# ScalarE makes the scattered token copies six ahead, with their extra column, in the expert part of an adaLN–Mamba–MoE block

## The chip, the cores and the metric

The kernel runs on one core of one Trainium2 chip. The metric is the device time of one execution in microseconds (us); the kernel before has a median of 2375.14 us over three runs (2374.47 to 2376.8). Engines are named as the profile names them: PE (TensorE, matrix products), DVE (VectorE), ACT (ScalarE), POOL (GpSimd), and SP (SyncE), whose queue issues most of the DMA transfers. [...]

## The reference

Two sequences of 2048 tokens with 256 channels pass through an adaptive layer norm and a bidirectional Mamba block, and then through a mixture of experts. Only the second half matters here:

```
h = layernorm(x) * (1 + cb) + sb
scores = softmax(h @ gate_w.T)                    # 8 experts
top_vals, idx = top_k(scores, 2)                  # two experts per token
xs = h[:, None, :] * weights[:, :, None]          # two scaled copies of each token
y = sum over experts e of mask_e * ((silu(xs@w1[e].T+b1[e]) @ w2[e].T + b2[e]) * (xs@w3[e].T + b3[e]))
z = silu(h @ sw1.T) * (h @ sw2.T) @ sw3.T         # shared expert, every token
out = x + gb * (y + z)
```

All arrays are float32. There are 2 x 2048 tokens and two copies of each, so 8192 rows of 256 numbers go to the experts.

## The kernel before, in words

The program has four stages. Up to about 1897 us of the profiled execution it runs the two Mamba directions. From about 1921 to 2076 us, which I call phase A, it opens the layer norm of both batches ("front" units), picks the experts of every token ("choose" and "rank" units on DVE), runs most of the shared expert (matmul groups `pg` and `pz` on PE), and scatters the first batch's token copies. From 2076 to about 2347 us, the expert stage, it runs 40 expert tiles of 256 rows. The last stage, to 2395 us, finishes the shared expert of the second batch and stores the output.

**How copies reach their experts.** For each batch there are 16 column blocks `j` and two ranks `n`, so 32 copies, each of 128 tokens on 128 partitions and 257 columns. ACT writes 256 columns: the normalised tokens times their expert weight (L1173). POOL writes the extra column 257 (L1176): a number, from `homes[b]`, from which the row is later computed to which the expert's result must return. POOL then issues an indirect DMA (L1177), which writes the 128 rows to the places `slots[b]` of the DRAM tensor `xs`. The copies live in a pool of eight buffers, so the ACT instruction that makes copy k has to wait until the DMA of copy k-8 has landed. `homes[b]` and `slots[b]` come from `route(b)` on DVE, whose last instruction of interest is L1145.

**Phase A's order** is written by hand: a list of 37 steps `k`, each with one shared-expert unit and some front units beside it. `follow(generator)` advances a generator by one yield. From step 17 on each step advances the first batch's scatter generator twice.

**The expert stage.** For tile i the SP queue loads three weight matrices, the biases and the tile's 256 rows `xg` from `xs` (`load_tile`, L1225 to L1229), three tiles ahead, each with four buffers. PE does `qh` (first product), `q` (third matrix), turns the next tile in (`qgT`), turns the last tile's result out (`qyT`), and does `q` again (second matrix, which needs `hT`). ACT applies silu to `qh` and writes `hT` (L1301), writes the third product with its bias (`x`, L1304), and copies the turned result to `outs` (L1273). DVE copies the turned-in tile `gT` (L1253) and multiplies the two products (L1311). At the end of tile i comes `sides(i)`: up to tile 7 it advances the second batch's scatter generator four times; from tile 9 (`NF` is 9) it sends finished tiles, two in a tile while there are several, each by two indirect DMAs from POOL (L1281) to the DRAM tensor `ys`.

**What orders scatters against loads.** Tiles 0 to 8 hold only rows of the first batch, so their loads are declared independent of the second batch's scatters. From tile 9 on the load of a tile must wait for all scatters that stand before it in the program, and a scatter that stands after a load must wait for that load. `load_tile(9)` stands in tile 6, before that tile's `sides`.

Of the kernel before, what the change touches and what calls it, by code (L numbers as in the profile page):

```python
# [8 lines left out]
F32 = mybir.dt.float32  # L9
AF = mybir.ActivationFunctionType  # L10
# [5 lines left out]
P = 128  # L16
NB, T, C = 2, 2048, 256
NJ = T // P
# [7 lines left out]
JC = TC // P  # L26
# [10 lines left out]
NF = -((E * (TS - 1) - 2 * T) // TS)  # L37
# [6 lines left out]
def kernel(  # L44
# [4 lines left out]
    nc = tc.nc  # L49
# [11 lines left out]
        out=flip, in_=flip, compare_op=ALU.not_equal, fill=1.0,  # L61
# [12 lines left out]
    xs_d = dram.tile([NT * TS, C + 1], F32, tag="xs", name="xs")  # L74
# [20 lines left out]
    x1s, xhs, mods = {}, {}, {}  # L95
# [47 lines left out]
    with tc.tile_pool(name="mw", bufs=1) as mw, tc.tile_pool(name="mw2", bufs=2) as mw2, \  # L143
# [44 lines left out]
        weights, state, ready, xns, accs = {}, {}, {}, {}, {}  # L188
# [359 lines left out]
        places = {}  # L548
# [307 lines left out]
        for s in range(NST + 4 + SPC):  # L856
            i, k = divmod(s, SPC)
# [41 lines left out]
            if i < NCH + 1:  # L899
# [3 lines left out]
                if k == 8 and 2 <= i < 2 + NB:  # L903
                    v = xs_d.rearrange("(p n) f -> p (n f)", p=P).rearrange("p (m k) -> p m k", k=NX)
                    n = slice((i - 2) * C // 2, C + 1 if i > 2 else C // 2)
# [30 lines left out]
    with tc.tile_pool(name="fw", bufs=1) as fw, tc.tile_pool(name="f1", bufs=1) as f1, \  # L936
# [44 lines left out]
        spare = fw.tile([P, 1], F32, tag="spare", name="spare")  # L981
# [5 lines left out]
        homes = [fw.tile([P, 2, NJ], F32, tag=f"home{b}", name=f"home{b}") for b in range(NB)]  # L987
# [8 lines left out]
        for v, pattern, base, each in ((filled, [[0, E], [TS, NK]], 0, 0), (tiles, [[1, NT], [0, NQ]], 0, 0),  # L996
# [4 lines left out]
            n = v.shape[1] * v.shape[2]  # L1001
# [3 lines left out]
        picks = {}  # L1005
# [68 lines left out]
                nc.vector.tensor_reduce(sc[:, n, js], got, AX.X, ALU.add)  # L1074
            yield

        slots, owners, left = {}, {}, {}

        def route(b):

# [80 lines left out]
        def apart(i, own, others, reason):  # L1161

            i = getattr(i, "ins", i)
            for group in others:
                tc.declare_no_dep(i, group=group, reason=reason)
            tc.add_to_no_dep_group(own, i)

        def scatter(b):
            sc = picks[b][1]
            for j in range(NJ):  # L1170
                for n in range(2):
                    v = f4.tile([P, C + 1], F32, tag="xs", bufs=8, name=f"xs{b}_{j}_{n}")
                    nc.scalar.activation(v[:, 0:C], xhs[b, j // JC][:, j % JC, :], AF.Copy,  # L1173
                                         scale=sc[:, n, j:j + 1])

                    nc.gpsimd.tensor_copy(v[:, C:C + 1], homes[b][:, n, j:j + 1])  # L1176
                    i = nc.gpsimd.indirect_dma_start(  # L1177
                        out=xs_d[:, :], in_=v, in_offset=None,
                        out_offset=bass.IndirectOffsetOnAxis(ap=slots[b][:, n, j:j + 1], axis=0))
                    apart(i, f"scatter{b}", (f"scatter{b}", f"load{b}"), "each writes rows of its own")  # L1180
                    yield

        def shared(b, q):

# [34 lines left out]
        def load_tile(i):  # L1219

            e = nc.sync.value_load(owners[i >= NF][0:1, i:i + 1], min_val=0, max_val=E - 1)
            ws = f4.tile([P, 3, KC, H], F32, tag="we", bufs=4, name=f"we{i}")
            xg = f4.tile([P, 2, C + 1], F32, tag="xg", bufs=4, name=f"xg{i}")
            for n, src in enumerate((w1, w3, w2)):
                nc.sync.dma_start(out=ws[:, n, :, :], in_=src[bass.ds(e, 1), :, :]  # L1225
                                  .rearrange("o (k p) h -> p (o k) h", p=P))
            bs = f4.tile([P, 3, KH], F32, tag="bs", bufs=4, name=f"bs{i}")
            nc.sync.dma_start(out=bs, in_=b123[:, :, bass.ds(e, 1), :].rearrange("p n o k -> p n (o k)"))
            d = nc.sync.dma_start(out=xg, in_=tiled(xs_d[i * TS:(i + 1) * TS, :]))  # L1229
            if i < NF:  # L1230
                apart(d, "load1", ("scatter1",), "full of the first batch's tokens")
            loaded[i] = ws, bs, xg

        def lin(ws, n, src, name):
            ps = bank(name).rearrange("p (m t) -> p m t", m=2)
            for m in range(KH):
                for k in range(KC):
                    nc.tensor.matmul(ps[:, m, :], ws[:, n, k, m * P:(m + 1) * P], src[:, k, :],  # L1238
                                     start=(k == 0), stop=(k == KC - 1))
            return ps  # L1240
# [8 lines left out]
        def turned_in(i):  # L1249
            xg = loaded[i][2]  # L1250
            ps = turn_tile(xg[:, :, 0:C], f"qgT{i}")
            gT = f2.tile([P, KC, TS], F32, tag="gT", name=f"gT{i}")
            nc.vector.tensor_copy(gT, ps)  # L1253
            nc.vector.scalar_tensor_tensor(xg[:, :, C], xg[:, :, C], float(i * TS), empty[:, 0, :],
                                           ALU.add, ALU.add)
            homeward[i] = f4.tile([P, 2], U32, tag="home", bufs=12, name=f"home{i}")
            nc.vector.tensor_copy(homeward[i], xg[:, :, C])
            return gT
# [27 lines left out]
        def expert_tiles(sides):  # L1286


            for i in range(3):
                load_tile(i)  # L1290
            gT, x3 = turned_in(0), None
            follow(routes[1])
            for i in range(NT):
                if i + 3 < NT:
                    load_tile(i + 3)
                ws, bs, _ = loaded.pop(i)
                hT = f2.tile([P, KH, TS], F32, tag="hT", name=f"hT{i}")
                y3 = f2.tile([P, KC, TS], F32, tag="x3", name=f"x3{i}")
                ps = lin(ws, 0, gT, f"qh{i}")
                for m in range(KH):  # L1300
                    nc.scalar.activation(hT[:, m, :], ps[:, m, :], AF.Silu, bias=bs[:, 0, m:m + 1])  # L1301
                ps = lin(ws, 1, gT, f"q3{i}")
                for m in range(KC):
                    nc.scalar.activation(y3[:, m, :], ps[:, m, :], AF.Identity, bias=bs[:, 2, m:m + 1])  # L1304
                if i + 1 < NT:
                    gT = turned_in(i + 1)
                if x3 is not None:
                    turned_out(i - 1, x3)
                ps = lin(ws, 2, hT, f"q2{i}")
                for m in range(KC):  # L1310
                    nc.vector.scalar_tensor_tensor(y3[:, m, :], ps[:, m, :], bs[:, 1, m:m + 1],  # L1311
                                                   y3[:, m, :], ALU.add, ALU.mult)
                x3 = y3
                sides(i)
            turned_out(NT - 1, x3)
# [27 lines left out]
        def store(b, q):  # L1343
            nc.sync.dma_start(out=tiled(out[b, q * TC:(q + 1) * TC, :]), in_=x1s[b, q])
# [5 lines left out]
        def part(b, q, n):  # L1350
            if n == LOAD:
                load_front(b, q)
            else:
                next(fronts[b, q], None)
# [3 lines left out]
        def unit(f):  # L1358
            e = f() if f else None
            while emptied:  # L1360
                emptied.pop(0)()
            if e:
                emptied.append(e)

        def follow(f):

            return next(f, 0) != 0
# [12 lines left out]
        def interleaved(keys):  # L1380

            units, due = [], []
            for k in keys:
                units += hidden[k][:2] + due + hidden[k][2:]
                due = result[k]
            return units + [None] + due
# [13 lines left out]
        scatters, routes = [scatter(0), scatter(1)], [route(0), route(1)]  # L1400
        for k, f in enumerate(interleaved([(0, 0), (0, 1), (0, 2), (0, 3), (1, 0), (1, 1)])):
            for p in beside.get(k, ()):
                part(*p)
            if k == 8:
                for v, w in iotas:
                    nc.vector.tensor_copy(v.rearrange("p a b -> p (a b)"), w)
            if k in (14, 16, 33):
                follow(routes[k // 33])
            unit(f)
            if k > 16:  # L1410
                for _ in range(2):
                    follow(scatters[0])
        while emptied:
            emptied.pop(0)()
        while follow(scatters[0]):
            pass

        twos = {}

        def sides(i):  # L1420
            for _ in range(4):
                follow(scatters[1])
            if i == 1:
                follow(routes[1])
            if i >= NF:
                for _ in range(2 if len(made) > 1 else 1):
                    send()
            for q in range(NTC):
                if i == N0 + 2 + 3 * q:
                    twos[q] = combine(0, q, fetch(0, q))  # L1430
                if N0 + 4 + 3 * q <= i <= N0 + 6 + 3 * q and not follow(twos[q]):
                    store(0, q)

        expert_tiles(sides)
        while made:
            send()
# [70 lines left out]
```

## Time and profile before

| what | value |
|---|---|
| median of three runs | 2375.14 us |
| profiled execution, its own time | 2396.49 us |
| span of the profiled execution | 2394.8 us |
| busy over the span: PE, DVE, ACT, POOL | 81%, 85%, 67%, 79% |
| expert stage up to tile 9 (2076 to 2140 us) | PE busy 61.96 of 64 us |
| tiles 10 and 11 (2140 to 2175 us) | PE busy 16.18 of 35 us |
| rest of the expert stage (2175 to 2347 us) | PE busy 171.90 of 172 us |

The profile is one execution, 21.35 us longer than the median of the runs without one. A timeline line gives the start in us, the duration in us, engine, source line, operation, output and input tiles, how many instructions are merged into the line, and in brackets how long the engine stood idle before it and what ended that idle time. `L1301` is line 1301 of the kernel. A line with x8 covers eight instructions.

### The profile page before, as it was taken

How to read it: one execution, taken by the hardware profiler on the slowest of the kernel's cores; microseconds unless marked ns; L12 is line 12 of the kernel's file. 1: busy time of each engine (PE TensorE's matmuls, PEld its weight loads, DVE VectorE, ACT ScalarE, POOL GpSimd, SP SyncE). 2: the span in 40 equal slices, each digit the busy share in tenths (PEclk: the TensorE clock that was granted, in tenths of full speed). 3: DMA queues.
4: the chain of work that ended last, by engine and by line, in shares of the span. 5: the costliest groups of instructions: out<-in, count | busy, mean ns of one | idle time of the engine just before them, and what ended most of it. 6: DMA issues, size and time to landing. Idle time of an engine off the chain costs nothing. (4 is left out here: it accounts for less than half of the span.)

```text
span 2394.8 us, 29909 instructions
## 1 busy us (share of the span) xinstructions
PE 1941.8 (81%) x9320; PEld 1333.1 (56%) x9320; DVE 2034.5 (85%) x2743; ACT 1599.9 (67%) x3345; POOL 1893.1 (79%) x1083
## 2 busy tenths in 40 slices
PE   5466878797978788887979788887876699987999
PEld 2133555554646555554556465555555555776885
DVE  5489999989999999999999999999999978622244
ACT  5557787768778787878787777878775344442331
POOL 0267898989999999999999999999999613564331
PEclk9678988888999899998889898999987899998999
DMA  4344448585444545445455445454446331466683
GB/s 161 107 156 159 145 166 199 189 213 182 152 168 164 166 153 185 156 159 168 141 171 172 159 153 170 155 160 160 145 166 217 101 121 43 146 200 197 215 291 144
DMA packets 230403, 393.70 MB, mean 164 GB/s; under 512 B 68162, under 2 KB 159810, under 8 KB 230244
## 3 DMA queue, kind: packets, MB, share of 16 engines
q1 hardware_dynamic: 222900, 371.30, 48.6%
q0 software_dynamic: 6912, 18.92, 2.1%
q8 instruction: 73, 1.20, 0.2%
q10 hardware_dynamic: 432, 1.58, 0.2%
q14 instruction: 86, 0.70, 0.1%
HBM read 340.27 MB, written 51.46 MB: 164 GB/s over the span
## 5 line engine op out<-in xcount | busy, mean ns | idle before, releaser
L461 POOL TENSOR_TENSOR db<-du,B 128x1024 f32<-128x1024 f32 x452 | 1061.2, 2366 | 18.2 <-DMA B<-bcs 10.8
L505 POOL TENSOR_TENSOR db<-h,C 128x1024 f32<-128x1024 f32 x252 | 597.4, 2371 | 65.8 <-issue 53.5
L480 ACT ACTIVATE da<-dt,w_a 128x512 f32<-128x512 f32 x904 | 594.7, 688 | 76.4 <-DVE dt L345 45.8
L527 PE MATMUL y<-ident,db 128*128 128x128 f32 x4096 | 566.5, 286 | 39.6 <-POOL db L505 37.2
L527 PEld LDWEIGHTS y<-ident,db 128*128 128x128 f32 x4096 | 503.7, 149 | 161.5 <-issue 101.1
L494 DVE TENSOR_TENSOR_SCAN da<-da,hl,db 128x512 f32<-128x512 f32 x460 | 562.8, 1268 | 4.9 <-POOL db L461 3.7
L494 DVE TENSOR_TENSOR_SCAN h<-da,hl,db 128x512 f32<-128x512 f32 x444 | 540.0, 1263 | 15.3 <-ACT da L480 15.3
L500 DVE TENSOR_TENSOR db<-da,C 128x512 f32<-128x512 f32 x460 | 292.1, 676 | 22.0 <-DMA C<-bcs 14.5
L281 PE MATMUL psc<-xp,w_conv 128*128 128x512 f32 x512 | 236.4, 605 | 10.2 <-ACT xp L270 6.4
L264 PE MATMUL psx<-xT,w_in 128*128 128x512 f32 x256 | 155.4, 727 | 102.7 <-ACT hl L515 90.1
L399 PE MATMUL psz<-w_in,xT 128*128 128x512 f32 x256 | 151.3, 723 | 56.3 <-ACT bT L362 36.3
L1281 POOL DMA_INDIRECT ys<-outs,home x80 | 76.7, 959 | 122.1 <-ACT outs L1273 112.3
L351 POOL TENSOR_TENSOR du<-dt,xc 128x512 f32<-128x512 f32 x64 | 81.3, 1271 | 98.4 <-DVE dt L345 98.4
L281 PEld LDWEIGHTS psc<-xp,w_conv 128*128 128x128 f32 x512 | 94.3, 194 | 108.3 <-issue 96.5
L298 PE MATMUL psd<-xc,w_x 128*48 128x512 f32 x128 | 96.8, 927 | 68.0 <-ACT hl L515 47.5
L427 PE MATMUL pso<-w_out,yg 128*128 128x256 f32 x512 | 118.6, 385 | 23.5 <-ACT e L321 22.2
L264 PEld LDWEIGHTS psx<-xT,w_in 128*128 128x128 f32 x256 | 49.8, 223 | 156.8 <-ACT hl L515 112.1
L1253 DVE COPY gT<-qgT 128x512 f32<-128x512 f32 x40 | 27.6, 691 | 113.3 <-PE qgT L947 82.7
L1301 ACT ACTIVATE hT<-qh,bs 128x256 f32<-128x256 f32 x80 | 33.5, 469 | 130.9 <-issue 75.9
L515 ACT COPY hl<-da 128x1 f32<-128x1 f32 x460 | 61.6, 157 | 87.6 <-DVE db L500 84.7
L427 PEld LDWEIGHTS pso<-w_out,yg 128*128 128x128 f32 x512 | 95.7, 192 | 39.1 <-ACT e L321 25.5
L1195 PE MATMUL pg<-fxT,s 128*128 128x512 f32 x256 | 115.3, 602 | 1.6 <-DVE hs L1201 0.7
(251 smaller groups left out, 3123.7 us busy)
## 6 DMA issues: line engine op xcount, KB each, us to landing
C<-bcs SPq DMA_DIRECT2D x256, 512.0 KB
B<-bcs SPq DMA_DIRECT2D x226, 512.0 KB
we<-in_w_dram SPq DMA_DIRECT2D x120, 256.0 KB
acc<-acc SPq DMA_DIRECT2D x32, 512.0 KB
xg<-xs SPq DMA_DIRECT2D x40, 257.0 KB
xn<-xn SPq DMA_DIRECT2D x16, 512.0 KB
two<-ys SPq DMA_DIRECT2D x16, 512.0 KB
xs<-blank SPq DMA_DIRECT2D x1, 5160.0 KB
```

What stands on the lines that cost most here:

```text
L264: nc.tensor.matmul(ps, w["in"][:, k, d * P:(d + 1) * P], v["xT"][:, k, :], start=(k == 0), stop=(k == KC - 1))
L281: nc.tensor.matmul(ps, w["conv"][:, d, k, :], v["xp"][:, d, k:k + TC], start=(k == 0), stop=(k == 3))
L298: nc.tensor.matmul(ps[:RK + 2 * NS, :], w["x"][:, d, :], v["xc"][:, d, :], start=(d == 0), stop=(d == ND - 1))
L399: nc.tensor.matmul(ps, v["xT"][:, k, j * P:(j + 1) * P], w["in"][:, k, DI:2 * DI], start=(k == 0), stop=(k == KC - 1))
L427: nc.tensor.matmul(ps[:, n, :], v["yg"][:, d, n * P:(n + 1) * P], wo[:, d, :], start=(d == 0), stop=(d == ND - 1))
L461: nc.gpsimd.tensor_tensor(db, bc(ready[i]["du"][:, d, :], NG), live["B", s // 2], ALU.mult)
L480: nc.scalar.activation(da[n], ready[i]["dt"][:, d, :], AF.Exp, scale=w["a"][:, d, m:m + 1])
L494: nc.vector.tensor_tensor_scan(h[n], da[n], x[n], hl[:, d, m:m + 1], ALU.mult, ALU.add)
L500: nc.vector.tensor_tensor(live["db", s][:, n, :], h, live["C", s // 2][:, n, :], ALU.mult)
L505: nc.gpsimd.tensor_tensor(live["db", s], live.pop(("h", s)), live["C", s // 2], ALU.mult)
L527: nc.tensor.matmul(ys["y"][j // 2][:, j % 2, d % 2 * P:(d % 2 + 1) * P], src[:, j * P:(j + 1) * P], ident, is_transpose=True, start=(first ...
L1195: nc.tensor.matmul(ps, s12[:, n, k, m * P:(m + 1) * P], xTs[b, q][:, k, :], start=(k == 0), stop=(k == KC - 1))
```

## The change

The scatter generator is split. It first makes six copies and yields after each; then, for each k, it makes copy k+6, writes the extra column of copy k on ACT, and issues the scatter of copy k from POOL. The extra column's POOL copy becomes an ACT copy of 128x1, and POOL gets a memset of a spare 128x1 tile in its place. In phase A the first batch's generator is advanced from step 14. After phase A the second batch's generator is advanced six times, and six times more at the start of the expert stage, ahead of tile 0. Sends begin in tile 7. The eight buffers stay.

```diff
         def scatter(b):
-            sc = picks[b][1]
-            for j in range(NJ):
-                for n in range(2):
-                    v = f4.tile([P, C + 1], F32, tag="xs", bufs=8, name=f"xs{b}_{j}_{n}")
-                    nc.scalar.activation(v[:, 0:C], xhs[b, j // JC][:, j % JC, :], AF.Copy,
-                                         scale=sc[:, n, j:j + 1])
-
-                    nc.gpsimd.tensor_copy(v[:, C:C + 1], homes[b][:, n, j:j + 1])
-                    i = nc.gpsimd.indirect_dma_start(
...
-                    yield
+            sc, ready = picks[b][1], []
+            places = [(j, n) for j in range(NJ) for n in range(2)]
+
+            def make(j, n):
+                v = f4.tile([P, C + 1], F32, tag="xs", bufs=8, name=f"xs{b}_{j}_{n}")
+                nc.scalar.activation(v[:, 0:C], xhs[b, j // JC][:, j % JC, :], AF.Copy,
+                                     scale=sc[:, n, j:j + 1])
+                ready.append(v)
+
+            for k in range(AHEAD):
+                make(*places[k])
+                yield
+            for k, (j, n) in enumerate(places):
+                if k + AHEAD < len(places):
+                    make(*places[k + AHEAD])
+                v = ready.pop(0)
+                nc.scalar.copy(v[:, C:C + 1], homes[b][:, n, j:j + 1])
+
+                nc.gpsimd.memset(spare, 0.0)
+                i = nc.gpsimd.indirect_dma_start(
...
+                yield
...
             follow(routes[1])
+            for _ in range(AHEAD):
+                follow(scatters[1])
             for i in range(NT):
...
-            if k > 16:
+            if k > 13:
                 for _ in range(2):
                     follow(scatters[0])
...
         while follow(scatters[0]):
             pass
+        for _ in range(AHEAD):
+            follow(scatters[1])
...
-            if i >= NF:
+            if i >= NF - 2:
                 for _ in range(2 if len(made) > 1 else 1):
                     send()
```

`AHEAD` is 6.

More of the change, by code (lines that the diff above doesn't have):

```diff
@@ L1075, in front @@
             yield
-        slots, owners, left = {}, {}, {}
+        slots, owners, left, AHEAD = {}, {}, {}, 6
         def route(b):
@@ L1168, in scatter @@
         def scatter(b):
-            sc = picks[b][1]
-            for j in range(NJ):
-                for n in range(2):
-                    v = f4.tile([P, C + 1], F32, tag="xs", bufs=8, name=f"xs{b}_{j}_{n}")
-                    nc.scalar.activation(v[:, 0:C], xhs[b, j // JC][:, j % JC, :], AF.Copy,
-                                         scale=sc[:, n, j:j + 1])
[L1176 to L1180, printed above, removed]
-                    yield
+            sc, ready = picks[b][1], []
[15 more added lines that the diff above has]
+                i = nc.gpsimd.indirect_dma_start(
+                    out=xs_d[:, :], in_=v, in_offset=None,
+                    out_offset=bass.IndirectOffsetOnAxis(ap=slots[b][:, n, j:j + 1], axis=0))
+                apart(i, f"scatter{b}", (f"scatter{b}", f"load{b}"), "each writes rows of its own")
+                yield
         def shared(b, q):
```

## The prediction

> **What bounds the kernel now.** I read the table of busy time by stage first, to see where PE does not work.
>
> ```profile
> 2076.00:2140.00 64.00, 61.96 (x328) 54.48 (x327) 26.85 (x77) 34.59 (x81) 35.30 (x60) 1.00 0.75 220
> 2140.00:2175.00 35.00, 16.18 (x62) 13.10 (x62) 3.61 (x10) 4.30 (x10) 24.71 (x46) 0.71 0.54 165
> 2175.00:2347.00 172.00, 171.90 (x898) 152.18 (x896) 62.06 (x149) 63.24 (x140) 60.65 (x113) 0.99 0.75 235
> ```
>
> The columns are the stretch, its length, busy time of PE, PE's weight loads, DVE, ACT and POOL, then granted clock, DMA share and GB/s. The expert stage is bound by PE except between 2140 and 2175 us. What stops it there stands in the timelines of SP, POOL and PE.
>
> ```profile
> 2124.23 0.38 SPq L1229 DMA_DIRECT2D xg<-xs  x1
> 2134.67 0.38 SPq L1229 DMA_DIRECT2D xg<-xs  x1
> 2145.63 0.38 SPq L1229 DMA_DIRECT2D xg<-xs  x1
> ```
>
> ```profile
> 2127.84 0.98 POOL L1177 DMA_INDIRECT xs<-xs,slot  x1 [4.99 <-ACT xs L1173]
> 2138.34 0.98 POOL L1177 DMA_INDIRECT xs<-xs,slot  x1 [4.96 <-ACT x L1304]
> ```
>
> ```profile
> 2148.65 1.12 PE L947 MATMUL qgT<-ident,xg 128*128 128x128 f32 x4 [4.76 <-DMA xg<-xs]
> ...
> 2150.41 3.62 PE L1238 MATMUL q<-hT,we 128*128 128x256 f32 x8
> ...
> 2173.40 3.78 PE L1238 MATMUL q<-hT,we 128*128 128x256 f32 x8 [10.79 <-ACT hT L1301]
> ```
>
> Loads of tiles 9, 10, 11 and the last eight scatters take turns: each waits for the other, 10.4 us a round where a tile takes PE 6.05 us (`qh` starts at 2083.61 and 2089.67). So tile 11's rows come 4.76 us late.
>
> The second stall, up to 2173.40, is of another kind.
>
> ```profile
> 2156.44 8.42 SPq L1225 DMA_DIRECT2D we<-in_w_dram  x3
> ```
>
> ```profile
> ACT hT L1301 <- remote: 21.6, 1, 21.6
> ```
>
> Three issues take SP 8.42 us (1.49 us in other tiles), ACT waits 21.6 us for a `qh` that PE finished at about 2156, and most semaphore records are missing there. PE would have gone on at about 2158.4; with its half-speed restart this costs 15.0 + 2.6 = 17.6 us. The profiled execution (2396.49 us, span 2394.8) is 21.35 us above the median run. I take this stall to belong to the profiled execution and leave it out of both sides; the median has then 3.7 us less in all the rest.
>
> **The change part by part.**
>
> *The point that decides.* Eight buffers, six copies ahead: copy k+6 takes the buffer of copy k-2. Its ACT instruction therefore waits until scatter k-2 has landed, and behind it in ACT's queue stands the extra column of copy k, which scatter k waits for. Before, the same wait was for the scatter eight back, and no line shows ACT waiting for it. So at most two scatters are now under way, and all that ACT does after the copy (`hT`, `x`, `outs`, silu) stands behind a landing. The durations:
>
> ```profile
> 2132.20 2.45 DMA xs<-xs,slot
> ```
>
> The chain of waits has 2.45 us for one scatter's landing. The semaphore records of the 32 scatters in phase A give 2.7 us on average from issue to last record, those of the 24 scatters from 2083 to 2122 us, beside tile loads, 4.0 us; those issued inside a burst of loads about 4.3. The Trainium skill (DMA: Bandwidth & Descriptors, section on the SWDGE path) fits a fixed 2.0 us plus bytes over 436 GB/s; for 128 x 1028 bytes that is an estimate of 2.3 us[...]. The measured rows decide: 2.7 quiet, 4.2 where a scatter meets loads.
>
> ```profile
> L515 ACT COPY hl<-da 128x1 f32<-128x1 f32 x460 | 61.6, 157 | 87.6 <-DVE db L500 84.7
> 2082.38 1.69 ACT L1173 ACTIVATE xs<-xh,sc 128x256 f32<-128x256 f32 x4
> ```
>
> The extra column on ACT: 0.157 us by the row, 0.2 with its issue. A copy of 256 columns: four in 1.69 us, 0.4 each. From ACT to the start of POOL's DMA 0.3 us (0.19 to 0.37 in POOL's rows). POOL's pace with a memset, as in sends, 1.27 us instead of 1.46: this gain is not on the path, as ACT sets the pace.
>
> *Tile 0.* Today:
>
> ```profile
> 2079.92 0.84 ACT L1301 ACTIVATE hT<-qh,bs 128x256 f32<-128x256 f32 x2 [11.40 <-PE qh L1238]
> 2082.78 0.18 POOL L1176 COPY xs<-home 128x1 f32<-128x1 f32 x1 [14.70 <-DVE home L1145]
> 2081.89 1.89 PE L1238 MATMUL q<-hT,we 128*128 128x256 f32 x8
> ```
>
> DVE has `homes` at 2082.7. Six scatters now stand ahead of `hT` on ACT. Column 0 is done at 2082.9; scatter 0 starts at 2083.2 and lands (2.7; the tile loads of 2069 to 2082 are done) at 2085.9; copy 8 and column 2 end at 2086.5; scatter 2 from 2086.8 lands at 2089.5; scatter 3, 1.27 later, lands at 2090.8; copy 11 and column 5 end at 2091.4, `hT` at 2092.2. `q` starts at 2092.3 instead of 2081.9: **10.4 us**. What is late next is everything, as PE has no other work.
>
> *Tiles 1 to 5.* `sides` puts four copies and columns before the next `hT`. The first two find their buffers free: to the first column 0.6 us, handover 0.3, landing 4.2, the other landing of the pair 1.27 later, one more copy and column 0.6: 7.0 us. With `hT` 0.84, `x` 0.84 and `outs` 0.5 ACT needs 9.2 us a tile; PE needs 6.05. Five such tiles: **15.8 us**. Bounds: landing 2.7 gives 7.7 us a tile and 8.2 in all, 4.8 gives 9.8 and 18.8. In tile 6 only two scatters are left, without a copy.
>
> *PE's clock.* After the 4.76 us of idle the rows above show `q` at 3.62 instead of 1.89 us, about 2.8 us lost with the products around it; after 0.88 us of idle nothing of size. The skill (TensorE: Matmul & The Clock Gate, part on the clock gate) says that an idle window of about 3.4 us halves the clock and that as much busy time restores it. Stalls of 3.2 us lie just under that. By the rule, no loss after tile 0; if each tile restarted cold it would be 5 x 2 = 10 us, but these lie under ACT's 9.2 us (cold PE reaches the next `qh` in 5.5 to 7 us). Only the last restart shows: 0 to 2, I take **1**.
>
> *What is gained.* At load 9, 30 of 32 scatters are issued; two wait for it, and rows for tiles 9 to 11 come more than a tile early. Gone are 4.76 and 2.8 us, and the smaller stalls of PE at 2114.84 (0.78, 0.3 for slower products) and 2137.61 (0.88): **9.6 us**.
>
> *Phase A.* The first six copies (2.4 us) fall into an idle time of 15.91 us on ACT before 2004.09, the second batch's six into the 11.40 us before 2079.92: nothing, as long as these exist. They let the first scatter start at about 2007.1 instead of 2007.50. But then the same two-deep chain holds, here with 2.7 us. I followed ACT's queue with the starts above: where two steps' pairs follow each other, ACT waits 1.5 to 3 us for landings, and what stands behind is late: `fxT` of chunk (1,1) by 3.4 us, of (1,2) by 5.0, silu of (1,0)'s last unit by 1.8, `fxT` of (1,3) by 4.1. PE's idle gaps and the work queued before them absorb most; of the last, PE's `fpsl` at 2053.88 moves to 2056.2: **2.4 us**, bounds 0 and 6. The last scatter of this batch goes out at about 2069.0 instead of 2067.10; load 0 has 4 us of room.
>
> *Sends two tiles sooner.* POOL has 60.65 of 172 us busy in the rest of the stage; no buffer of `outs` is reused before tile 12. Path: 0. They are moved ahead of nothing but other sends; if POOL lagged they would cost nothing before a fetch at tile 26.
>
> Sum: 10.4 + 15.8 + 1 - 9.6 + 2.4 = 20.0 us, against the profile's own 2396.49 and so also against the median: 2375.1 + 20 = **2395 us**.
>
> **The rivals.**
>
> *Landings stay quiet.* With ACT slower, the loads are spread over longer tiles, and 2.7 us holds everywhere: 10.4 + 8.2 + 1 - 9.6 + 1 = 11, so 2386 us. For it: scatters outside bursts land in 2.3 to 2.9 us. Against: in the new order the deciding pair starts about 2 us after `hT`, just as the next weights' buffers come free.
>
> *Phase A is bound by ACT too.* DVE stands on the path there and waits in order for silu. If every late ACT result reaches PE, phase A loses up to 10 us and tiles run at 9.8: 10.4 + 18.8 + 2 - 9.6 + 10 = 32, so 2407 us. Against: several gaps of 2 to 4 us on DVE.
>
> *Not slower.* The long stall of 2151 to 2173 us is in every run, and it comes from the burst of twenty sends without a pause that starts at 2143.99. Sends from tile 7 on could be spread and the stall vanish: 2395 - 17.6 = 2377 us, no change that can be told; with landings of 2.7 us, 2386 - 17.6 = 2368, faster. It decides once the stall gives back over 15 us. For it: SP, ACT and DVE all stop during that burst. Against: the 21.35 us between profile and median, and that the new order again has some seven finished tiles waiting when POOL begins to send.
>
> **How the numbers follow.** Main case 0.55 (its own range 2388 to 2403), quiet landings 0.17, phase A bound 0.10, not slower 0.18, of which faster 0.10 and within 0.2% 0.08; 0.2% (4.8 us) is about what a measurement of this kernel can tell from no change. Slower by over 0.2% is the first three, 0.82. The range of 2377 to 2406 leaves out the faster cases, half of the unchanged, and the top of phase A's: about 0.19.
>
> **What would show it.** ACT's `hT` of tile 0 would start near 2091 on this clock with a DMA before it, and PE's first second-matrix `q` be idle some 10 us for `hT`; tiles 1 to 5 would start `qh` every 8 to 9.5 us; ACT's copies would show idle time ended by scatter DMAs, which today is 0.0; no `qgT` would wait for `xg` at tiles 9 to 11. The prediction is wrong if `hT` of tile 0 is within 3 us of its old place after `qh`, if tiles 1 to 5 keep 6.05 us, or if the stall during the sends is in the runs and goes.

## The result, and the profile after

The changed kernel takes 2400.8 us (median of four runs, 2399.34 to 2402.55) where the kernel before takes 2374.8 (2373.1 to 2376.8): 26.0 us more, ratio 1.0109 (1.0092 to 1.0127). A second measurement, beside other experiments, gave 2404.1 us against 2375.93, ratio 1.012 (1.0103 to 1.0136). The profiled execution of the changed kernel took 2401.75 us, its span is 2399.8.

The busy time by stage, columns as in the prediction:

```profile
2076.00:2150.00 74.00, 55.10 (x247) 46.58 (x246) 21.68 (x61) 28.60 (x91) 31.18 (x57) 0.86 0.55 171
2150.00:2180.00 30.00, 30.00 (x160) 26.71 (x159) 9.17 (x25) 11.51 (x27) 20.25 (x39) 1.00 0.81 250
2180.00:2347.00 167.00, 167.00 (x886) 148.59 (x885) 61.31 (x149) 62.62 (x138) 63.64 (x120) 1.00 0.78 246
```

PE's idle time has moved. Before, it was at tiles 10 and 11; now it is in the first tiles, 18.9 of 74 us, and from 2150 us on PE never stops. PE's timeline says what it waited for:

```profile
2084.35 1.99 PE L1250 MATMUL qh<-gT,we 128*128 128x256 f32 x8 [0.38 <-DVE gT L1265]
...
2098.39 3.78 PE L1250 MATMUL q<-hT,we 128*128 128x256 f32 x8 [9.87 <-ACT hT L1315]
...
2106.91 1.99 PE L1250 MATMUL q<-hT,we 128*128 128x256 f32 x8 [0.38 <-ACT hT L1315]
...
2116.74 3.78 PE L1250 MATMUL q<-hT,we 128*128 128x256 f32 x8 [3.52 <-ACT hT L1315]
...
2135.62 3.21 PE L1250 MATMUL q<-hT,we 128*128 128x256 f32 x8 [3.63 <-ACT hT L1315]
```

Every gap but the first, which is as long in the kernel before, ends with ACT's `hT`. Why `hT` is late stands in ACT's own timeline, here in tiles 0 and 2:

```profile
2089.22 0.19 ACT L1186 COPY xs<-home 128x1 f32<-128x1 f32 x1 [11.45 <-DVE home L1145]
...
2092.26 0.51 ACT L1175 ACTIVATE xs<-xh,sc 128x256 f32<-128x256 f32 x1 [2.37 <-DMA xs<-xs,slot]
...
2097.86 0.83 ACT L1315 ACTIVATE hT<-qh,bs 128x256 f32<-128x256 f32 x2
...
2114.77 0.51 ACT L1175 ACTIVATE xs<-xh,sc 128x256 f32<-128x256 f32 x1 [4.55 <-DMA xs<-xs,slot]
2115.18 0.17 ACT L1186 COPY xs<-home 128x1 f32<-128x1 f32 x1
...
2116.22 0.83 ACT L1315 ACTIVATE hT<-qh,bs 128x256 f32<-128x256 f32 x2
```

ACT stands idle ahead of a copy (L1175) until a scatter has landed, and the column (L1186) goes at once after it. What comes later in the program waits behind them: `hT` (L1315) of tile 2, whose `qh` PE started at 2108.74, begins at 2116.22, when the last copy and column are through. ACT's waits between 2076 and 2160 us (total, how many, the longest) hold a line that the kernel before did not have:

```profile
ACT xs L1175 <- DMA xs<-xs,slot: 31.4, 19, 4.5
```

The loads of tiles 9, 10 and 11 hardly take turns with scatters any more: one turn is left, the last two scatters between the first two loads. In SP's timeline the loads of rows of tiles 10 and 11 come 8.1 and 3.9 us after the one before, ahead of PE's need. The weights' issues keep their 1.5 us, so the long stall is absent from this execution.

```profile
2154.20 0.38 SPq L1241 DMA_DIRECT2D xg<-xs  x1
...
2162.34 0.38 SPq L1241 DMA_DIRECT2D xg<-xs  x1
...
2166.28 0.60 SPq L1241 DMA_DIRECT2D xg<-xs  x1
...
2167.89 1.50 SPq L1237 DMA_DIRECT2D we<-in_w_dram  x3
```

### The profile page after: what moved, and what is told of

It is laid out like the page before. It is cut to its first block, busy times and chain, and to the rows that moved or that the text cites. A ratio compares the mean times of both kernels' runs of the same rounds, so it can differ in the third digit from the quotient of the medians.

```text
span 2399.8 us, 29964 instructions
## 1 busy us (share of the span) xinstructions
PE 1954.0 (81%) x9320; PEld 1340.4 (56%) x9320; DVE 2034.4 (85%) x2743; ACT 1608.5 (67%) x3409; POOL 1884.7 (79%) x1083
## 5 line engine op out<-in xcount | busy, mean ns | idle before, releaser
L1189 POOL DMA_INDIRECT xs<-xs,slot x64 | 64.9, 1014 | 154.0 <-DVE hs L1213 72.0
L399 PEld LDWEIGHTS psz<-w_in,xT 128*128 128x128 f32 x256 | 54.6, 236 | 105.4 <-issue 43.5
## 6 DMA issues: line engine op xcount, KB each, us to landing
xs<-blank SPq DMA_DIRECT2D x1, 5160.0 KB, 25.6
```

The costliest lines, as they stand in the source:

```text
L399: nc.tensor.matmul(ps, v["xT"][:, k, j * P:(j + 1) * P], w["in"][:, k, DI:2 * DI], start=(k == 0), stop=(k == KC - 1))
```

## The experiments

**The level of the kernel before.** The experiments ran in four sets, each beside its own runs of the kernel before, which took 2396.4 us in the first set (2391 to 2400, 26 runs), 2375.9 in the second (2371 to 2379, 19), 2377.0 in the third (2373 to 2380, 16) and 2396.5 in the fourth (2393 to 2400, 9). Within a set every run lies on one level. The first two sets were on the same chip. The traces give the difference a place: in the first and fourth sets each of them has the long stall of the prediction (its second stall), in the others none has it. (The kernel before itself was traced in the first set alone.) The first measurement has both: its timed runs of the kernel before lie on the lower level, its profile with the stall on the upper. I therefore read ratios within a set only, and compare stretches from trace to trace:

| kernel (set) | `fxT` of chunk (1,0) to `qgT` of tile 0 | tile 0 | tiles 1 to 5 | tiles 6 to 11 | ratio to before (95%) |
|---|---|---|---|---|---|
| before, first profile | 92.2 | 5.7 | 31.2 | 62.1 with the stall | |
| before_again (1) | 92.2 | 5.7 | 32.6 | 60.5 with the stall | 1.0000 (0.9991 to 1.0009) |
| slowsend (2) | 92.2 | 5.7 | 30.3 | 43.8 | 1.0001 (0.9991 to 1.0010) |
| the change, first profile | 99.7 | 17.6 | 44.6 | 36.3 | 1.0109 (1.0092 to 1.0127) |
| after_again (2) | 99.8 | 17.7 | 44.4 | 36.3 | 1.0120 (1.0103 to 1.0136) |
| ahead0 (1) | 92.2 | 5.7 | 35.8 | 55.8 with the stall | 1.0005 (0.9996 to 1.0014) |
| swap (1) | 94.2 | 16.5 | 39.6 | 53.7 with the stall | 1.0053 (1.0036 to 1.0070) |
| poolcol (1) | 92.2 | 17.3 | 36.9 | 51.4 with the stall | 1.0035 (1.0023 to 1.0047) |
| only1 (2) | 92.2 | 17.7 | 45.5 | 36.3 | 1.0082 (1.0065 to 1.0099) |
| only0 (2) | 99.9 | 5.7 | 30.3 | 39.7 | 1.0023 (1.0014 to 1.0033) |
| ahead3 (3) | 92.2 | 8.3 | 30.3 | 37.1 | 0.9987 (0.9975 to 0.9999) |
| send9 (3) | 100.0 | 17.5 | 45.9 | 37.3 | 1.0106 (1.0090 to 1.0123) |
| early32 (3) | 92.2 | 5.7 | 31.4 | 36.3 | 0.9967 (0.9955 to 0.9979) |
| ahead5 (4) | 92.9 | 13.9 | 35.2 | 55.2 with the stall | 1.0025 (1.0012 to 1.0038) |

The first column is in us from the start of ACT's `fxT` of chunk (1,0) (1984.12 in the first profile of before) to the start of the first `qgT` (2076.35). `fxT` is the turned block of tokens that the gate's products (`fpsl`) and the shared expert's (`pg`) read; chunk (1,0) is the first quarter of the second batch. The other columns are differences of `qh` starts: first to second, second to seventh, seventh to thirteenth. Six tiles at 6.05 us would be 36.3. From the thirteenth `qh` to the end of the span all traces without the stall take 216.9 us. The start of the first column varies from trace to trace, 1979.4 to 1985.6, whatever the kernel; the change has two copies ahead of it, but ACT is idle for 3.14 us between them and `fxT` (after_again). So all that the change does happens in these four stretches.

In the sets with the stall, tiles 1 to 5 are not clean either. Of ahead0's 35.8 us, 5.2 are lost in one tile where ACT stands idle with nothing named that ended the wait, and where no copy waits for a landing:

```profile
2105.84 0.84 ACT L1315 ACTIVATE hT<-qh,bs 128x256 f32<-128x256 f32 x2 [6.28 <-issue]
```

So in rows with the stall this column is an upper bound of what the edit costs there.

**before_again: the kernel before, unchanged.**

> The kernel before, unchanged, profiled a second time. Theory (the long stall of 2151 to 2173 us belonged to one profiled execution): no stall of ACT for qh of more than 10 us while the sends run, the profiled execution within 5 us of 2375, and in its expert stage only the wait of PE for the rows of tile 11, about 5 us, with a slow restart of about 3 us. Rival (the burst of sends causes it): the stall of about 20 us is there again, though the changed kernel, with a burst of 24 sends, did not have it.

It took 2396.3 us, and its trace has the stall at the same place. Its waits between 2076 and 2175 us, and SP's timeline:

```profile
ACT hT L1301 <- remote: 21.7, 1, 21.7
```

```profile
2157.38 8.46 SPq L1225 DMA_DIRECT2D we<-in_w_dram  x3
...
2173.94 1.49 SPq L1225 DMA_DIRECT2D we<-in_w_dram  x3
```

What follows: the stall does not belong to one profiled execution, as I had taken it, but to a whole set of runs. The 2375 us of the first measurement and of the second set are the level without it.

**ahead0: no copies ahead, the rest of the change kept** (column on ACT, memset, sends sooner).

```diff
-        slots, owners, left, AHEAD = {}, {}, {}, 6
+        slots, owners, left, AHEAD = {}, {}, {}, 0
...
-            if k > 13:
+            if k > 16:
```

> The changed kernel with AHEAD = 0 and the first batch's scatters from step 17 on: the extra column stays on ACT with POOL's memset, sends stay two tiles sooner, but each copy is made directly ahead of its scatter, so a copy's buffer is that of the scatter eight back. Theory (the loss is the wait for the scatter two back): ACT hardly waits for scatters, phase A and tiles 0 to 5 are as in the kernel before, the turns of loads and scatters at tiles 9 to 11 are back: 2375, between 2370 and 2380. Rival (the columns on ACT, or the sends sooner, cost the time): 2390 or more.

2396.95 us beside 2396.39: no difference (the 2375 expected was for the level without the stall). Phase A and tile 0 stand as before, and ACT's copies wait for no landing. The column on ACT, the memset in its place and the sooner sends cost nothing that can be told without the copies ahead; only0 below, in a set without the stall, has them in its second batch with tiles 1 to 5 at 30.3 us.

**swap: the column and the scatter of copy k ahead of the making of copy k+6.**

```diff
-                if k + AHEAD < len(places):
-                    make(*places[k + AHEAD])
                 v = ready.pop(0)
                 nc.scalar.copy(v[:, C:C + 1], homes[b][:, n, j:j + 1])
...
+                if k + AHEAD < len(places):
+                    make(*places[k + AHEAD])
```

> The changed kernel with one order exchanged: column and scatter of copy k stand ahead of the making of copy k+6. Theory: scatter k no longer waits for the landing of scatter k-2, three are under way instead of two, but ACT still stops for each landing: 1.3 us less at tile 0, about 0.6 us less in each of tiles 1 to 5, 1 to 3 us less in phase A: 2395, between 2391 and 2398. Rival (the number under way doesn't matter, ACT's extra work does): 2401 as before, within 2 us.

2407.38 us, 11 more than before in this set. Phase A loses 2.0 us instead of 7.5, a larger gain than the 1 to 3 us expected; tiles 1 to 5 take 39.6 instead of 44.4; tile 0 gains 1.2 (16.5 instead of 17.7), as expected. So the column behind the waiting copy is the larger part of phase A's loss and a third or more of that of tiles 1 to 5, but not of tile 0's: there the copies themselves, which wait ahead of `hT`, suffice.

**poolcol: the column back on POOL, six ahead kept.**

```diff
-                nc.scalar.copy(v[:, C:C + 1], homes[b][:, n, j:j + 1])
-
-                nc.gpsimd.memset(spare, 0.0)
+                nc.gpsimd.tensor_copy(v[:, C:C + 1], homes[b][:, n, j:j + 1])
```

> The changed kernel with the extra column written by POOL again (its copy of 128x1 in place of the memset), all else kept, six ahead. Theory: scatter k needs nothing from ACT but a copy made long ago, so POOL goes at its own pace of 1.46 us; ACT still waits for landings, but at POOL's pace, 5.8 us for four, under PE's 6.05 us a tile. Tile 0 keeps its loss of about 10 us, tiles 1 to 5 lose at most 5 us together instead of 16, phase A loses 2 to 4 instead of 7.5: 2383, between 2378 and 2389. Rival (any wait of ACT for landings costs what was seen): 2395 or more.

2403.78 us, 7.4 more than before in this set. Phase A loses nothing, where 2 to 4 us were expected; tile 0 still takes 17.3 us; tiles 1 to 5 take 36.9. PE's two waits of size in those tiles, 1.18 and 2.82 us, are of the kind that ahead0 has: ahead of the second, ACT's `hT` stands idle 5.28 us with nothing named, and no landing ends either. ACT's waits in phase A (1995 to 2082 us):

```profile
ACT xs L1175 <- DMA xs<-xs,slot: 4.6, 4, 2.3
```

With the column on POOL the scatters no longer wait for ACT, their pace is POOL's, and most landings have come by the time that ACT asks. The making ahead alone is harmless in phase A, and harmful at tile 0, where the scatters can start only with `homes` and the second six copies, each behind a landing, stand ahead of `hT`.

**after_again: the change, in a set without the stall.**

> The changed kernel once more, on the chip of the first four runs, where the kernel before took 2396.4 us in every run and its trace holds the long stall of about 20 us beside the burst of sends. If the stall belongs to the kernel before and its burst (theory A, the change takes it away because its scatters end later and slower): this kernel shows no stall, its 24 sends follow each other while TensorE works on, and it takes 2401 us as at first, a ratio of 1.002. If the stall belongs to the chip or the moment (theory B): it comes here too, and the time is 2396 + 24 = 2420 us, a ratio of 1.010 as at first. In both the eight tiles show the alternation of 6.8 and 11 us and tile 0 waits some 10 us for hT.

2404.1 us against 2375.93. What theory A rests on falls: the stall does not belong to the kernel before and its burst, since in this set the kernel before, by its time and by the trace of its near copy slowsend below, has none either. The ratio is that of the first measurement because neither side had it. Whether the changed kernel has the stall in a set of the other level was not run; its relatives poolcol, swap and ahead5 have it there.

**only1 and only0: the early copies in one batch alone.**

```diff
-        slots, owners, left, AHEAD = {}, {}, {}, 6
+        slots, owners, left, AHEADS = {}, {}, {}, (0, 6)
...
-            if k > 13:
+            if k > 16:
```

(with `AHEADS[b]` in place of `AHEAD`; only0 has (6, 0) and keeps k > 13)

> Early copies for the second batch alone (none ahead in the first, whose scatters begin at unit 17 as before; second batch six ahead, column on ScalarE, sends two tiles sooner). My theory: phase A's slip was the first batch's copies on ScalarE ahead of fxT, so qgT of tile 0 comes at about 2074 to 2077 us as in the kernel before instead of 2082.8, while tile 0 still waits 10 us for hT and tiles 1 to 6 take 16 us more than six times 6.05. The span is 6.5 us under that of the changed kernel run beside it. Rival: the slip of phase A comes from the column and the memset, not from the early copies; then qgT(0) is at 2082 us here too and nothing is won over the changed kernel.

> Early copies for the first batch alone (second batch none ahead: each copy, its column and its scatter in turn; sends two tiles sooner). My theory: phase A slips as in the changed kernel (qgT of tile 0 some 6 us later than in the kernel before, at about 2081 us), tile 0's q for hT follows qgT(0) in about 6 us, not 15.6, and tiles 1 to 6 run at 6.1 us but for one refill wait; so about 20 us under the changed kernel up to tile 6, of which the turns of loads and scatters at tiles 9 to 11 give back about 5 to 10. Rival: tiles 1 to 6 are slow because of the column on ScalarE, not because of the copies standing six ahead of their landings; then they take 50 us here too.

The change comes apart. Only1 takes 2396.0 us, +20.1: phase A as before, tile 0 and tiles 1 to 5 as in the change. Only0 takes 2381.4 us, +5.5: phase A 7.7 us longer, the tiles at 6.05 us, one wait for tile 11's rows left (3.13 us, where slowsend below has 5.28). Its one trace gives 3.6 us by its stretches. Together 25.6, against 28.2 for both. Neither rival holds. Only1 is 8.1 us under the changed kernel, where 6.5 was expected. Only0 is 26 us under it from the first `qh` to the seventh, where some 20 was expected, and the turns give back 3.4 of them, less than the 5 to 10 expected. Phase A in only0, by ACT's timeline:

```profile
2037.03 0.51 ACT L1175 ACTIVATE xs<-xh,sc 128x256 f32<-128x256 f32 x1 [2.71 <-DMA xs<-xs,slot]
2037.53 1.06 ACT L1038 COPY fxT<-fpsT 128x512 f32<-128x512 f32 x2
```

`fxT` of chunk (1,2) comes right behind a copy that waited 2.71 us for a landing. In poolcol, the same place:

```profile
2028.83 1.07 ACT L1038 COPY fxT<-fpsT 128x512 f32<-128x512 f32 x2 [1.08 <-PE fpsT L947]
```

There `fxT` waits for PE, as it should, and comes 8.7 us earlier (the two kernels' `fxT` of chunk (1,0) were 0.6 us apart, at 1980.56 and 1981.11).

**slowsend: the kernel before with two more memsets ahead of each send.**

```diff
             for j in range(2):
-                nc.gpsimd.memset(spare, 0.0)
+                for _ in range(3):
+                    nc.gpsimd.memset(spare, 0.0)
```

> The kernel before with two more memsets of the spare column ahead of each send, so that sends follow each other at about 1.9 us instead of 1.27. If the long stall is made by the burst of sends back to back (every instruction of SyncE takes 0.70 us in it): it is gone or shorter, and the time falls to 2376 to 2385 us, a ratio of 0.992 to 0.996. If the stall is not made by the density of the burst: it stays, it lasts as long as the longer burst (38 us instead of 25), and the time is 2396 to 2410 us, a ratio of 1.000 to 1.006.

Inconclusive on the stall: it ran in a set without one, and took 2375.75 us, as the kernel before did there (its sends were 1.77 us apart on average). But its trace is the nearest thing to a trace of the kernel before without the stall, and shows what the turns of loads and scatters cost by themselves:

```profile
2133.40 1.89 PE L1238 MATMUL qh<-gT,we 128*128 128x256 f32 x8
...
2142.29 1.11 PE L947 MATMUL qgT<-ident,xg 128*128 128x128 f32 x4 [5.28 <-DMA xg<-xs]
...
2146.89 1.89 PE L1238 MATMUL qh<-gT,we 128*128 128x256 f32 x8
```

13.5 us between these two `qh` instead of 6.05, so 7.4 us, and no other gap up to there.

**ahead3 and ahead5: another distance.** Copy k+3 takes the buffer of scatter k-5, copy k+5 that of scatter k-3.

```diff
-        slots, owners, left, AHEAD = {}, {}, {}, 6
+        slots, owners, left, AHEAD = {}, {}, {}, 3
...
-            if k > 13:
+            if k > 14:
```

(ahead5 changes the number alone)

> The changed kernel with three copies ahead instead of six (first batch's scatters from unit 15), all else the same. My theory (the harm is the distance: copy k+6 takes the buffer of scatter k-2, which has just been issued, so ScalarE's queue stands behind a landing; copy k+3 takes that of scatter k-5): tile stage from the first qh to the twelfth 72 to 77 us instead of 92.4, tile 0's wait for hT 3 us instead of 10, phase A's slip under 1 us instead of 7.5; the time 2376 to 2381 us beside a kernel before of 2376. Rival: the harm is the number of copies and columns ahead of hT on ScalarE whatever their distance; then half of the loss stays, 2390 us.

> The changed kernel with five copies ahead: copy k+5 takes the buffer of scatter k-3, so three scatters can be under way instead of two; all else the same. Theory (the tile is as long as its four landings divided by the scatters under way, 4 x 4.2 / 3 = 5.6 us, and 2.2 us for hT, x and outs on ScalarE): tiles 1 to 5 take 7.8 us each instead of 9.2, tile 0 waits 6 to 7 us for hT instead of 10, first to twelfth qh 79 to 84 us (92.4 with six ahead, 69.6 with three), phase A slips 2 to 5 us; the time 2385 to 2392 us beside 2376. Rival: the harm has an edge (GpSimd's own pace of 1.27 us a scatter already covers a landing of 2.6 us twice over, so three under way are as good as five): 70 to 73 us in that stretch, the time 2374 to 2379 us.

ahead3 takes 2374.4 us beside 2377.0, just under the range expected: with the same instructions as the change in another order, the loss is gone. Phase A slips by 0.0, tile 0 waits 2.30 us for `hT`, tiles 1 to 5 run at 6.05, and the stretch from the first to the twelfth `qh` is 69.6 us, under the 72 expected, since the turns cost PE only 0.57 us now:

```profile
2085.61 1.99 PE L1250 MATMUL q<-hT,we 128*128 128x256 f32 x8 [2.30 <-ACT hT L1315]
...
2146.13 0.66 PE L947 MATMUL qgT<-ident,xg 128*128 128x128 f32 x4 [0.57 <-DMA xg<-xs]
```

ahead5 lies between: tile 0 waits 6.12 us for `hT`, as expected; tiles 1 to 5 take 35.2 / 5 = 7.0 us each, where 7.8 was expected and 8.9 is the changed kernel's; phase A slips 0.7 instead of 2 to 5. Up to the seventh `qh` it loses 13.7 us against slowsend, the change 33.7. Its set has the stall on both sides (of the kernel before by its times alone), so its 6.3 us over the kernel before cannot be set beside the 9 to 16 expected without it.

```profile
2089.87 3.78 PE L1250 MATMUL q<-hT,we 128*128 128x256 f32 x8 [6.12 <-ACT hT L1315]
```

The waits of ACT for landings in phase A (1995 to about 2083 us), from the waits of each trace, and the slip of phase A go together: 3.2 us and 0.0 (ahead3), 4.6 and 0.0 (poolcol), 9.6 and 0.7 (ahead5), 11.9 and 2.0 (swap), 20.1 and 7.5 (the change, second trace). In these five, some ten us of waiting are covered, and most of what comes above them is paid.

**send9: the change with sends from tile 9 on.**

```diff
-            if i >= NF - 2:
+            if i >= NF:
```

> The changed kernel with the sends from tile 9 on as in the kernel before. My theory: the two tiles cost and bring nothing, since the sends stand behind the scatters in GpSimd's queue either way: 2404 us as the changed kernel beside 2376, within 2 us. Rival: the sooner sends (4 to 8 more of them in the burst) delay the tile loads: then 5 us less than the changed kernel.

2403.35 us beside 2377.0, ratio 1.0106; the changed kernel had 1.0109 and 1.0120. The sooner sends do nothing that can be told.

**early32: a version that beats both.** None ahead, column on ACT; all 32 scatters of the second batch stand before the load of tile 9.

```diff
-        slots, owners, left, AHEAD = {}, {}, {}, 6
+        slots, owners, left, AHEAD = {}, {}, {}, 0
...
-            if k > 13:
+            if k > 16:
...
-            for _ in range(4):
+            for _ in range(6 if i < 2 else 5):
                 follow(scatters[1])
```

> None ahead in either batch, column on ScalarE and memset as in the changed kernel, sends two tiles sooner; but 6, 6, 5, 5, 5, 5 scatters of the second batch in tiles 0 to 5 instead of 4 in each of eight, so that all 32 stand before the load of tile 9 and no load and scatter have to take turns. Theory: the wait of 7.4 us between the qh of tile 10 and that of tile 11 (13.5 us apart instead of 6.05) goes; GpSimd's 32 scatters at 1.27 us end 46 us after the first qh, their last landing and the load of tile 9 fit before its turn at 53 us. First to twelfth qh 66.6 to 69 us instead of 73.7, the time 2369 to 2372 us, a ratio of 0.997 to 0.998. Rival: five or six copies a tile put ScalarE behind landings again (scatters closer than the ring of eight carries): each tile takes 6.5 to 7 us for six tiles, and the gain is used up, 2374 to 2378 us. If the long stall is there in all runs as in the first four, both this kernel and the one before take 20 us more.

2370.1 us beside 2377.0, ratio 0.9967 (0.9955 to 0.9979), and 67.4 us from the first `qh` to the twelfth, both as expected. POOL's last scatter and SP's next loads of rows, tiles 9 and 10:

```profile
2123.71 0.96 POOL L1189 DMA_INDIRECT xs<-xs,slot  x1 [0.19 <-issue]
```

```profile
2127.51 0.38 SPq L1241 DMA_DIRECT2D xg<-xs  x1
...
2131.09 0.61 SPq L1241 DMA_DIRECT2D xg<-xs  x1
```

The last scatter starts 45.5 us after the first `qh` (2078.21), the load of tile 9 3.8 us later, and PE does not wait for rows. The `qh` of tiles 10 and 11 follow each other at PE's own pace:

```profile
2139.55 1.89 PE L1250 MATMUL qh<-gT,we 128*128 128x256 f32 x8
...
2145.61 1.89 PE L1250 MATMUL qh<-gT,we 128*128 128x256 f32 x8
```

It gives up 1.1 us in tiles 1 to 5, where five or six copies a tile make ACT wait for landings a little (7.9 us in all, most of it covered), and gains 7.4 at tile 11: 6.3 of the 6.9 us measured. The gain that the change was able to make was there to be had by moving scatters, without any copy ahead.

## Why the prediction was right, and where it was not

The forecast was 2395 us, +20; measured were +26.0 and +28.2. By its own steps, with the second trace of the change (after_again) against slowsend as the kernel before without the stall:

| step | predicted | measured |
|---|---|---|
| tile 0 | 10.4 | 12.0 |
| tiles 1 to 5, with the restart of PE | 16.8 | 14.2 |
| gained at tiles 9 to 11 | -9.6 | -7.4 |
| phase A | 2.4 (0 to 6) | 7.5 |
| sends sooner | 0 | 0 |
| sum | 20.0 | 26.2 |

(The terms are rounded, the sum is of the unrounded.) The expert stage came out near its forecast, 18.8 us against 17.6, in part by luck: tile 0 and the gain were 1.6 and 2.2 us worse than forecast, tiles 1 to 5 were 2.6 better. Most of what is missing is in phase A.

- *The point that decides* held. Ahead3 has the same instructions at another distance and loses nothing in all, ahead5 lies between, and the waits for landings appear in ACT's list as foretold.
- *Tile 0.* `hT` was predicted to be 10.4 us late; the product that needs it starts 15.58 us after `qgT` instead of 5.54, so 10.0. The restart of PE at half speed (3.78 instead of 1.89 us for that product) makes 12.0 of it. I had put one such restart, 1 us, at the end of the row of tiles; most of it is here.
- *Tiles 1 to 5.* 8.9 us a tile instead of 9.2. Landings were 3.4 us on average between 2083 and 2148 us (first trace, the records of 28 scatters, from issue to the last), not 4.2. That is the direction of the rival "landings stay quiet", though not down to its 2.7. That the spread of the loads shortened them is not shown by itself. The 4.0 read for the kernel before is likely too low: in its trace most of those scatters have 2 to 7 of their 16 landing records. Slowsend, whose records are complete, gives 4.7 for the same 24 scatters. After the fact, the simpler form that I used for ahead5, four landings divided by the scatters under way plus 2.2 us, gives 9.0 with 3.4 for two scatters (8.9 measured) and 6.7 for three (7.0 measured).
- *What is gained.* The large wait is gone, 7.4 us with the slower products behind it (the parts forecast add to 9.5, not 9.6). The smaller stalls of PE at 2114.84 and 2137.61, 2 us of the 9.6, stood in traces of the level with the long stall; slowsend has neither.
- *Phase A* is the term that was mis-sized, beyond its upper bound. I foresaw `fxT` of chunks (1,1), (1,2) and (1,3) late by 3.4, 5.0 and 4.1 us, and gaps of PE absorbing most. They were late by 4.4, 8.9 and 6.8 (second trace, counted from `fxT` of (1,0)), and nothing was absorbed: `qgT` of tile 0 came 7.5 us late. Two things were wrong. A landing that holds a copy also holds the column of an older one and so the next scatter, so that one late step makes all later ones late until the ACT queue runs dry; my walk let the queue catch up between steps. And gaps of PE that are already used up by the first lateness do not absorb the second. That the lateness reaches PE appears in its timeline of the second trace, where `fpsl` of chunk (1,2) waits for `fxT`; in the kernel before this `fpsl` has no wait and takes 1.85 us:

```profile
2041.93 3.64 PE L1044 MATMUL fpsl<-wg,fxT 128*128 128x8 f32 x16 [3.96 <-ACT fxT L1038]
```

That phase A loses its 7.5 us by the landings on ACT is shown by only0, poolcol, swap and ahead3, and swap puts 5.5 of them down to the column behind the waiting copy; how the two reasons share what was mis-sized is argued only.

- *The rival "not slower"* rested on the long stall being in every run. It was not in the runs of the first measurement, so leaving it out on both sides was right for that sum, but my reason, that it belongs to the profiled execution alone, was wrong: in two sets it is in every trace, and by their times in every run.
- *PE's clock.* The forecast that stalls of 3.2 us leave the clock alone did not hold: stalls from 2.42 us on were followed by slow products in some places, and one of 3.81 us was not (last section). In tiles 1 to 5 the second trace of the change has one such restart, which is inside the 14.2 us; the first trace has two.
- *"Phase A bound by ACT too"* had the truth in its first half (7.5 of its 10 us) and not in the second (tiles at 9.8 us).

## What to carry to other kernels

A ring of n buffers filled m ahead leaves n - m transfers under way (one more where the transfer is issued ahead of the next copy, as in swap). Making copies earlier out of the same ring shortens the time that a transfer has to land, and what stands behind the copy on the maker's engine waits for landings too. Before work is put ahead, count the distance between a buffer's writer and the transfer that frees it, and compare it with a landing in the traffic of that stage: here, with eight buffers, three ahead cost nothing that can be told and six ahead cost 26 us. And when a profile shows a wait made by the order of instructions (loads and scatters that take turns), move the instructions that take turns, not the work ahead of them.

## What the runs showed of the hardware that was not expected

*The long stall* comes and goes by sets of runs, on the same chip too, and then it is in all traces of the set. In before_again, from about 2149.6 to 2173.7 us nearly each record of SP's queue is 0.70 to 0.73 us or twice that after the one before, branch and register instructions too, while PE goes on with the products whose inputs it has and POOL issues a send every 1.27 us. It begins 5 us after the first send of the burst (2144.88) and ends 4 us after the last one (2169.9). In poolcol the burst starts at 2138.56, and pauses after 2155.02; the stall is over at 2158.9. In the sets of the lower level bursts just as dense (24 sends at 1.27 us in the change) do no harm. So the burst may be needed, but is not enough; what else it takes is open. One more thing goes with it: each of the six traces with the stall holds 13,700 to 14,100 landing records, each of the eight without it about 15,670. So the recording of the trace may have a part in the state; no run here separates the two. In the kernel before it costs 20.5 us (2396.4 against 2375.9 on the same chip).

*PE's restart.* In the first trace of the change, idle times of 3.52, 3.63 and 9.87 us were followed by products of 3.78, 3.21 and 3.78 us in place of 1.89. The Trainium skill (TensorE: Matmul & The Clock Gate, part on the clock gate) states an idle window of about 3.4 us before the clock is halved. The length of an idle time alone does not decide it here, as only1 and send9 show:

```profile
2122.01 3.47 PE L1250 MATMUL q<-hT,we 128*128 128x256 f32 x8 [2.42 <-ACT hT L1315]
```

```profile
2120.10 1.99 PE L1250 MATMUL q<-hT,we 128*128 128x256 f32 x8 [3.81 <-ACT hT L1315]
```

What the traces show is where the idle time lies. In all fourteen the granted clock is 1.00 or 0.50 and changes only at points that are a multiple of 3.41 us apart. In the expert stage, a step of 3.41 us at full clock was followed by half clock when PE was idle for 2.02 us of it or more (27 steps), and by full clock when it was idle for 1.99 us or less (989 steps). The 2.42 us of only1 put 2.02 into one step; the 3.81 us of send9 were split into 1.98 and 1.83. This is read from this case's products alone; in phase A two steps with 0.42 and 0.50 us of idle were followed by half clock too.

*Landings.* The same 128 x 1028 bytes took, from issue to the last record in the first trace of the change, 2.7 us on average in phase A (at most 3.9) and 3.4 in the expert tiles beside the tile loads (2.4 to 5.5).
